# Float32r scores in one pass of 32 rows, and exponentials over three PSUM banks

## The chip, the cores and the metric

The kernel runs on one core of a Trainium2 chip. The metric is the device time of one execution in microseconds. Before the change it took 10,427.56 us (median of 3 runs, 10,423.74 to 10,437.85).

Names of engines in the profile: PE is TensorE (PEld its weight loads), ACT is ScalarE, DVE is VectorE, POOL is GpSimd, and SP is SyncE, which issues most of the DMAs here. PSUM has eight banks of 512 float32 columns on 128 partitions. PE writes its results there and the other engines fetch them.

## The reference

Four images of 64 x 64 pixels with 128 channels go through two layers, all in float32.

```python
# layer 0: gated convolutions and causal attention, one head of 4 (q, k) and 16 (v) dims
c1 = conv_same(elu(x), W1, b1)
a, b = split(conv_same(c1, W2, b2), 2)
c3 = a * sigmoid(b)
q, k, v = c3 @ Wq + bq, c3 @ Wk + bk, c3 @ Wv + bv
x = x + c3 + tile(causal_softmax(q @ k.T / 4) @ v, 8) @ W3 + b3
# layer 1: t holds 4096 tokens of 128 dims
y = layernorm(t); q, k, v = y @ wq, y @ wk, y @ wv      # 16 heads of 8 dims
h = y + (softmax(q @ k.T) @ v) @ wo                     # no mask: 4096 x 4096 scores a head
t = t + h + (silu(h @ w1) * (h @ w3)) @ w2
y = layernorm(t)                                        # 8 experts, the best two of each token
t = t + sum_of_top2(softmax(y @ router_w + router_b), y @ expert_w + expert_b)
```

Most of the arithmetic is in layer 1's attention: 4 images x 16 heads x 4096 x 4096 scores, one exponential for each, and their weighted sums.

## The kernel before

`fast_path` computes one image after the other. Exponentials are taken of the bare scores; at the end a verdict on the largest queries, keys and values says whether that was safe, and only if not does `general_path` compute everything again. Here it does not.

Per image the stages are `l0_convs` (L244 to L308), `l0_attention` (scores L402, exponentials L415 and L418, sums L381, `project` L358), the transposes of the normalised tokens, `l1_attention` (from L430), `l1_ffn` (L567) and `l1_experts` (L601).

**Layer 1's attention.** Its first part projects queries and keys for eight blocks of 512 tokens (L438, L439). To keep float32 accuracy with bf16 products, `three_terms` (L235 to L242) splits the result into three bf16 terms: an ACT cast, a DVE subtraction, a POOL cast and another DVE subtraction. The terms go to DRAM (`d_k`, `d_q`) and come back with each row in the right place: for each of four heads (NSLOT), 24 rows at partition 32j. The rows of keys are the 8 dims times 3 key terms. The rows of queries hold one dim three times, so that one matmul over 24 rows multiplies one query term with all three key terms. Three matmuls into the same PSUM columns (L546, i = 0, 1, 2) give all nine products.

The main loop walks 32 blocks: four groups g of four heads, and for each eight blocks c of 512 queries. In each block it takes 32 steps kt, one per 128 keys. A step has
- 12 bf16 score matmuls of 24 rows x 128 keys x 512 queries (three terms, four heads; the heads stand in different 32-row groups of the array), into two tiles of two PSUM banks each,
- two exponentials of 128 x 1024 (L556) on ACT,
- four float32 sums `acc += v1.T @ e` (L509; two matmul instructions each in the trace), one per head, in four 32-column groups of the array. Their 9 rows are a row of ones and 8 dims of v, so that the softmax's denominator comes along.

The sums lag LAG = 2 steps behind the scores. At a block's end DVE copies `acc` to SBUF (L524). Two steps later `by_token` transposes it on PE (L495) and normalises on DVE (L498, L500). Keys of the next group (`keys`, four DMAs) and queries of the next block (`queries`, four DMAs) are loaded one ahead into second buffers by SP.

**PSUM.** One bank holds `acc`, one is `m_tile` for small products and transposes, and six belong to the pool `ps_s`: three buffers of two banks. All stages take their tiles from it by `s_tile()`: convolutions, layer 0's scores and its projection, the FFN's two products (L583, L584), the experts' products (L666, which DVE adds up in L675).

**What orders the work.** A framework orders the instructions of each engine, and it puts a semaphore wait ahead of an instruction where a buffer that it reads or writes is still in use by another engine. Which buffer a tile gets is settled by its pool. Each engine works through its own list in order; a waiting instruction holds up those behind it.

Of the kernel before, what the change touches and what calls it, by code (L numbers as in the profile page):

```python
# [8 lines left out]

FP = mybir.dt.float32  # L10
BF = mybir.dt.bfloat16
AF = mybir.ActivationFunctionType
ALU = mybir.AluOpType
AX = mybir.AxisListType

P = 128
C = 128
IMG = 64
N = IMG * IMG
NT = N // P  # L20
QB = 512
NQ = N // QB
# [4 lines left out]
SLOT = 32  # L27
NSLOT = P // SLOT
# [5 lines left out]
HIDDEN = 344  # L34
FCH = [(0, 128), (128, 128), (256, 88)]
NE = 8

NTERM = 3  # L40
# [49 lines left out]
def fast_path(ctx: ExitStack, tc: tile.TileContext, a: dict, where: dict, out: bass.AP, verdict):  # L90
# [2 lines left out]
    x = a["x"]  # L93
    B = x.shape[0]
    LAG = 2

    const = ctx.enter_context(tc.tile_pool(name="f_const", bufs=1))
    big = ctx.enter_context(tc.tile_pool(name="f_big", bufs=1))
    ep = ctx.enter_context(tc.tile_pool(name="f_ep", bufs=8))
    wk = ctx.enter_context(tc.tile_pool(name="f_wk", bufs=2))  # L100
    sm = ctx.enter_context(tc.tile_pool(name="f_sm", bufs=2))
    dram = ctx.enter_context(tc.tile_pool(name="f_dram", bufs=2, space=bass.MemoryType.DRAM))
    ps_s = ctx.enter_context(tc.tile_pool(name="f_ps_s", bufs=3, space=bass.MemoryType.PSUM))
    ps_o = ctx.enter_context(tc.tile_pool(name="f_ps_o", bufs=1, space=bass.MemoryType.PSUM))
    ps_m = ctx.enter_context(tc.tile_pool(name="f_ps_m", bufs=1, space=bass.MemoryType.PSUM))

    def s_tile():
        return ps_s.tile([P, 1024], FP, tag="s", name="s")

    def m_tile():  # L110
        return ps_m.tile([P, QB], FP, tag="m", name="m")

    def e_tile():
        return ep.tile([P, 1024], FP, tag="e", name="e")


    n_fast = where["head_sum"][1]
# [116 lines left out]
    def three_terms(src):  # L234

        xs = wk.tile([P, NTERM, 1024], BF, tag="x", name="x")
        rest = e_tile()
        nc.scalar.copy(xs[:, 0, :], src)
        nc.vector.tensor_tensor(rest, src, xs[:, 0, :], ALU.subtract)
        nc.gpsimd.tensor_copy(xs[:, 1, :], rest)  # L240
        nc.vector.tensor_tensor(xs[:, 2, :], rest, xs[:, 1, :], ALU.subtract)
        return xs  # L242
# [186 lines left out]

    def l1_attention(b, yT, h):  # L430

        d_k = dram.tile([P, NTERM, N], BF, tag="k1", name="d_k1")
        d_q = dram.tile([NQ, P, NTERM, QB], BF, tag="q1", name="d_q1")
        top = sm.tile([P, 2, NQ], FP, tag="top", name="top")
        for c in range(NQ):
            cols = slice(c * QB, (c + 1) * QB)
            ps = s_tile()
            nc.tensor.matmul(ps[:, :QB], lhsT=wq1, rhs=yT[:, cols], start=True, stop=True)  # L438
            nc.tensor.matmul(ps[:, QB:], lhsT=wk1, rhs=yT[:, cols], start=True, stop=True)  # L439
            nc.vector.tensor_reduce(  # L440
                top[:, :, c], ps.rearrange("p (j n) -> p j n", j=2), AX.X, ALU.max, apply_absolute_value=True
            )
            terms = three_terms(ps)
            nc.sync.dma_start(out=d_k[:, :, cols], in_=terms[:, :, QB:])
            nc.sync.dma_start(out=d_q[c], in_=terms[:, :, :QB])

        tops = sm.tile([P, 2], FP, tag="tops", name="tops")
        nc.vector.tensor_reduce(tops, top, AX.X, ALU.max)
        nc.vector.tensor_tensor(seen[:, 2, b : b + 1], tops[:, 0:1], tops[:, 1:2], ALU.mult)
        nc.vector.tensor_scalar(seen[:, 2, b : b + 1], seen[:, 2, b : b + 1], 1e30, None, ALU.min)  # L450

        top_v = sm.tile([P, NT // 8], FP, tag="topv", name="topv")
        for s in range(NT // 8):
            ps = s_tile()
            for k in range(8):
                i = 8 * s + k
                nc.tensor.matmul(
                    ps[:, k * P : (k + 1) * P], lhsT=yT[:, i * P : (i + 1) * P], rhs=wv1, start=True, stop=True
                )
            nc.vector.tensor_copy(  # L460
                v1[:, 8 * s : 8 * s + 8, :, 1:], ps.rearrange("p (k h d) -> p k h d", h=NH1, d=HD1)
            )
            nc.vector.tensor_reduce(top_v[:, s : s + 1], ps, AX.X, ALU.max, apply_absolute_value=True)
        nc.vector.tensor_reduce(seen[:, 3, b : b + 1], top_v, AX.X, ALU.max)


        rows = HD1 * NTERM

        def keys(g):
            kx = big.tile([P, N], BF, tag="kx", bufs=2, name="kx")  # L470
            for j in range(NSLOT):
                head = NSLOT * g + j
                src = d_k[head * HD1 : (head + 1) * HD1].rearrange("d y n -> (d y) n")
                nc.sync.dma_start(out=kx[j * SLOT : j * SLOT + rows, :], in_=src)
            return kx

        def queries(g, c):

            qx = wk.tile([P, NTERM, QB], BF, tag="qx", name="qx")
            for j in range(NSLOT):  # L480
                head = NSLOT * g + j
                src = d_q[c][head * HD1 : (head + 1) * HD1].rearrange("d x n -> d (x n)")
                nc.sync.dma_start(
                    out=qx[j * SLOT : j * SLOT + rows].rearrange("p x n -> p (x n)"),
                    in_=src.unsqueeze(1).to_broadcast([HD1, NTERM, NTERM * QB]),
                )
            return qx

        nt = big.tile([P, NT, C], FP, tag="y", name="nt")

        def by_token(g, c, at):

            ps = m_tile()
            for k in range(4):
                nc.tensor.transpose(ps[:, k * P : (k + 1) * P], at[:, k * P : (k + 1) * P], ident)  # L495
            pj = ps.rearrange("p (k j s) -> p k j s", j=NSLOT, s=SLOT)
            rc = sm.tile([P, 4, NSLOT], FP, tag="rc", name="rc")
            nc.vector.reciprocal(rc, pj[:, :, :, 0])  # L498
            gc = slice(g * NSLOT * HD1, (g + 1) * NSLOT * HD1)
            nc.vector.tensor_tensor(  # L500
                nt[:, 4 * c : 4 * c + 4, gc].rearrange("p k (j d) -> p k j d", d=HD1),
                pj[:, :, :, 1 : 1 + HD1],
                rc.unsqueeze(3).to_broadcast([P, 4, NSLOT, HD1]),
                ALU.mult,
            )

        def add_up(g, c, kt, es):
            for j in range(NSLOT):
                nc.tensor.matmul(  # L509
                    acc[j * SLOT : j * SLOT + 1 + HD1, :],  # L510
                    lhsT=v1[:, kt, NSLOT * g + j, :],
                    rhs=es[j // 2][:, (j % 2) * QB : (j % 2 + 1) * QB],
                    start=kt == 0,
                    stop=kt == NT - 1,
                )

        order = [(g, c) for g in range(NG1) for c in range(NQ)]
        ready = []

        def finish(n, kt, es):  # L520
            add_up(*order[n], kt, es)
            if kt == NT - 1:
                at = wk.tile([P, QB], FP, tag="at", name="at1")
                nc.vector.tensor_copy(at, acc)  # L524
                ready.append(at)
            if kt == 1 and ready:
                by_token(*order[n - 1], ready.pop())

        kx, qx = keys(0), queries(0, 0)
        kx_next = qx_next = None  # L530
        late = []
        for n, (g, c) in enumerate(order):
            if n:
                qx = qx_next
                if c == 0:
                    kx = kx_next
            if n + 1 < len(order):
                qx_next = queries(*order[n + 1])
            if c == 0 and g + 1 < NG1:
                kx_next = keys(g + 1)  # L540
            for kt in range(NT):
                ss = [s_tile(), s_tile()]
                for i in range(NTERM):
                    for j in range(NSLOT):
                        r = slice(j * SLOT, j * SLOT + rows)
                        nc.tensor.matmul(  # L546
                            ss[j // 2][:, (j % 2) * QB : (j % 2 + 1) * QB],
                            lhsT=kx[r, kt * P : (kt + 1) * P],
                            rhs=qx[r, i, :],
                            start=i == 0,  # L550
                            stop=i == NTERM - 1,
                        )
                es = []
                for ps in ss:
                    e = e_tile()
                    nc.scalar.activation(e, ps, AF.Exp)  # L556
                    es.append(e)
                late.append((n, kt, es))
                if len(late) > LAG:
                    finish(*late.pop(0))  # L560
        for item in late:
            finish(*item)
        by_token(*order[-1], ready.pop())
        return nt

# [847 lines left out]
```

## Time and profile before

| | us |
|---|---|
| median of 3 runs | 10,427.56 |
| the profiled execution | 10,433.93 |
| its span | 10,432.1 |
| PE busy | 9,972.6 |
| ACT busy | 8,198.4 |
| DVE busy | 1,150.2 |
| the four attentions of layer 1, first to last exponential | 4 x 1,932 |

A stage is a stretch of the timeline. In the first image the convolutions take until about 245 us, layer 0's attention until 376, the projection until 418, layer 1's attention until 2,352, the FFN until 2,500 and the experts until 2,627; the next images repeat this every 2,600 us.

In a group of the profile, the text before the bar is line, engine, operation, result and operands, shapes and count; behind it are busy time in us and the mean ns of one; behind the second bar is the idle time of the engine just before these instructions, and what ended it. The durations of neighbouring instructions on PE and ACT overlap somewhat, so that the distance of two starts is shorter than one duration. PEclk or "granted clock" is the share of TensorE's full clock that the chip granted.

### The profile page before, as it was taken

The numbers are of one execution on the slowest core, as the hardware profiler recorded it, in microseconds if no ns is written. First come the engines' busy times: TensorE is split into PE (matmuls) and PEld (weight loads), VectorE is DVE, ScalarE is ACT, GpSimd is POOL, SyncE is SP. The second block draws the span as 40 slices with busy tenths as digits, with TensorE's granted clock in tenths as the row PEclk, the third lists the DMA queues.
The fourth block names the chain that finished last, engine by engine and source line by source line (L and its number), as shares of the span: only waits on it lengthen the run. The fifth ranks groups of instructions, "written<-read, shape, count | busy, mean of one in ns | idle before, by whom it ended". The sixth has DMA issues, their size and how long they took to land.

```text
span 10432.1 us, 204188 instructions
## 1 busy us (share of the span) xinstructions
PE 9972.6 (96%) x90561; PEld 3179.9 (30%) x90565; DVE 1150.2 (11%) x3539; ACT 8198.4 (79%) x8965; POOL 184.3 (2%) x177
## 2 busy tenths in 40 slices
PE   8899999997989999999798999999979899999997
PEld 4322222224432222222442222222244222222224
DVE  1200000004220000000412000000051200000005
ACT  1699999991169999999116999999911799999991
POOL 0000000000000000000000000000000000000000
PEclk9999999998999999999889999999988999999998
DMA  1100000000010000000001000000000100000000
GB/s 26 35 6 10 6 9 7 6 5 15 5 34 6 10 6 9 7 6 5 16 4 35 7 9 6 10 6 6 5 16 4 35 7 9 6 10 6 6 5 9
DMA packets 86914, 112.51 MB, mean 11 GB/s; under 512 B 8835, under 2 KB 71779, under 8 KB 84195
## 3 DMA queue, kind: packets, MB, share of 16 engines
q1 hardware_dynamic: 83267, 97.59, 3.2%
q8 instruction: 710, 11.63, 0.5%
q10 hardware_dynamic: 2752, 1.77, 0.1%
q14 instruction: 185, 1.52, 0.0%
HBM read 64.99 MB, written 34.34 MB: 10 GB/s over the span
## 4 chain that ended last, share of the span: by engine, by line
PE 93%; DVE 4%; DMA 1%; ACT 1%; issue 0%; SPq 0%; POOL 0%; DVEq 0%; ACTq 0%; POOLq 0%
PE acc L509 38%; PE s L546 35%; PE s L291 5%; PE s L276 2%; PE s L666 2%; PE acc L381 2%; DVE t L675 2%; PE s L402 1%; PE s L583 1%; PE s L584 1%; PE m L495 1%; PE m L592 1%; PE m L231 1%; PE s L367 1%; PE m L574 0%
## 5 line engine op out<-in xcount | busy, mean ns | idle before, releaser
L556 ACT ACTIVATE e<-s 128x1024 f32<-128x1024 f32 x8192 | 7642.7, 1022 | 149.5 <-PE s L546 149.5
L509 PE MATMUL acc<-e,f_v 128*9 128x512 f32 x32768 | 4296.2, 595 | 4.5 <-ACT e L556 4.5
L546 PE MATMUL s<-qx,kx 24*128 24x512 bf16 x49152 | 3926.0, 377 | 29.5 <-DMA kx<-d_k 28.5
L546 PEld LDWEIGHTS <-kx 24*128 24x128 bf16 x49152 | 1548.0, 91 | 3823.5 <-issue 3467.2
L509 PEld LDWEIGHTS acc<-e,f_v 128*9 128x9 f32 x32768 | 486.7, 88 | 1753.4 <-issue 1687.1
L524 DVE COPY at<-acc 128x512 f32<-128x512 f32 x128 | 88.6, 692 | 7149.6 <-PE acc L509 7149.6
L291 PE MATMUL s<-c,f_w2c 128*128 128x512 f32 x1152 | 499.9, 592 | 0.0
L666 PE MATMUL s<-f_we,e 128*128 128x512 f32 x512 | 313.1, 763 | 58.2 <-DVE t L675 53.2
L299 ACT ACTIVATE e<-s,f_b 128x512 f32<-128x512 f32 x32 | 22.0, 687 | 422.8 <-PE s L291 422.7
L675 DVE SCALAR_TENSOR_TENSOR t<-s,gate,t 128x128 f32<-128x128 f32 x1024 | 305.9, 343 | 5.3 <-PE s L666 2.5
L291 PEld LDWEIGHTS s<-c,f_w2c 128*128 128x128 f32 x1152 | 215.5, 189 | 263.5 <-issue 263.5
L418 ACT ACTIVATE e<-s 128x1024 f32<-128x1024 f32 x224 | 217.6, 1021 | 91.1 <-PE s L402 90.4
L276 PE MATMUL s<-e,f_w1c 128*128 128x512 f32 x576 | 249.9, 596 | 3.1 <-DVE t L675 1.9
L402 PE MATMUL s<-qk 36*128 36x512 bf16 (+1 forms) x576 | 169.3, 388 | 76.0 <-DMA qk<-d_q 74.1
L655 ACT COPY g<-m 8x512 f32<-8x512 f32 x32 | 18.4, 575 | 230.4 <-PE m L653 230.4
L232 ACT COPY e<-m 128x512 f32<-128x512 f32 x64 | 37.5, 586 | 204.4 <-PE m L231 204.4
L381 PE MATMUL acc<-e,f_v 128*17 128x512 f32 (+3 forms) x1152 | 197.7, 600 | 0.0
L586 ACT ACTIVATE e<-s 128x512 f32<-128x512 f32 (+1 forms) x96 | 56.8, 596 | 165.6 <-PE s L584 165.5
L588 POOL TENSOR_TENSOR t<-t,h 128x512 f32<-128x512 f32 x32 | 40.5, 1266 | 8117.7 <-DVE h L577 8117.7
L666 PEld LDWEIGHTS s<-f_we,e 128*128 128x128 f32 x512 | 118.7, 247 | 202.9 <-issue 120.9
L283 ACT ACTIVATE c<-s,f_b 128x1024 f32<-128x1024 f32 x16 | 17.9, 1118 | 186.7 <-PE s L276 186.7
L276 PEld LDWEIGHTS s<-e,f_w1c 128*128 128x128 f32 x576 | 109.2, 190 | 141.7 <-issue 141.0
(146 smaller groups left out, 2962.0 us busy)
## 6 DMA issues: line engine op xcount, KB each, us to landing
qx<-d_q SPq DMA_DIRECT2D x512, 72.0 KB
d_k<-x SPq DMA_DIRECT2D x32, 384.0 KB
d_q<-x SPq DMA_DIRECT2D x32, 384.0 KB
kx<-d_k SPq DMA_DIRECT2D x64, 192.0 KB
t<-in_x_dram SPq DMA_DIRECT2D x16, 512.0 KB
out_dram<-t SPq DMA_DIRECT2D x32, 256.0 KB
f_w2c<-in_L_conv_W_dram ACTq DMA_DIRECT2D x1, 1152.0 KB
qk<-d_q SPq DMA_DIRECT2D x12, 96.0 KB
```

Of the source, the lines that this page charges most:

```text
L231: nc.tensor.transpose(ps[:, k * P : (k + 1) * P], src[:, k, :], ident)
L276: nc.tensor.matmul(rows(ps[:, h * QB : (h + 1) * QB]), lhsT=w1c[:, tap, :], rhs=e0[:, r0 : r0 + 8, kx : kx + IMG], start=(tap == 0), stop= ...
L291: nc.tensor.matmul(rows(ps[:, h * QB : (h + 1) * QB]), lhsT=w2c[:, tap, h * C : (h + 1) * C], rhs=c1[:, 8 * c + ky : 8 * c + ky + 8, kx : ...
L367: nc.tensor.matmul(ps[:, k * C : (k + 1) * C], lhsT=l_, rhs=w3f, start=True, stop=True)
L381: nc.tensor.matmul(acc[j * SLOT : j * SLOT + 1 + DV0, off:], lhsT=v0[:, kt, :], rhs=e[:, lo:hi], start=r == 0, stop=r == c,)
L402: nc.tensor.matmul(ps[:, lo:hi], lhsT=kx[:kr, kt * P : (kt + 1) * P], rhs=qx[:kr, c * QB + off : (c + 1) * QB], start=True, stop=r < c,)
L418: nc.scalar.activation(e, ps, AF.Exp)
L509: nc.tensor.matmul(acc[j * SLOT : j * SLOT + 1 + HD1, :], lhsT=v1[:, kt, NSLOT * g + j, :], rhs=es[j // 2][:, (j % 2) * QB : (j % 2 + 1) * ...
L546: nc.tensor.matmul(ss[j // 2][:, (j % 2) * QB : (j % 2 + 1) * QB], lhsT=kx[r, kt * P : (kt + 1) * P], rhs=qx[r, i, :], start=i == 0, stop= ...
L556: nc.scalar.activation(e, ps, AF.Exp)
L666: nc.tensor.matmul(px[:, h * QB : (h + 1) * QB], lhsT=yT[:, k * P : (k + 1) * P], rhs=we_f[:, h * QB : (h + 1) * QB], start=True, stop=True,)
L675: nc.vector.scalar_tensor_tensor(tk, px[:, n * C : (n + 1) * C], gate[:, k, n : n + 1], tk, ALU.mult, ALU.add)
```

## The change

- Queries and keys are split into two terms of the type float32r (`FR`; four bytes): an ACT copy that rounds, and a DVE subtraction. The POOL cast and one of the two DVE subtractions go. `d_k` and `d_q` hold four-byte values; `d_q` is written twice over.
- Rows: 8 dims x 2 key terms x 2 make 32 rows per head, which hold all four products of the terms. One matmul of 32 rows replaces the three of 24 rows. The four heads fill all 128 rows.
- Keys of a group come in four DMAs of a quarter of the tokens each, into one buffer `kx` instead of two. Queries of a block come in one DMA.
- Scores are numbered through over heads, steps and blocks, and taken three at a time (WIDE = 3): three scores into three neighbouring PSUM banks, one exponential of 128 x 1536. A triple can span two steps or two blocks. There are 5,464 exponentials instead of 8,192. A step's four sums are issued when the score of its last head is handed over. The buffers for exponentials are five of 1536 columns instead of eight of 1024.
- The six PSUM banks are one tile, `banks`, for the whole kernel. `s_tile(n)` gives the next n banks of it in turn. All stages use it.

```diff
-    ep = ctx.enter_context(tc.tile_pool(name="f_ep", bufs=8))
+    ep = ctx.enter_context(tc.tile_pool(name="f_ep", bufs=5))
...
-    ps_s = ctx.enter_context(tc.tile_pool(name="f_ps_s", bufs=3, space=bass.MemoryType.PSUM))
+    ps_s = ctx.enter_context(tc.tile_pool(name="f_ps_s", bufs=1, space=bass.MemoryType.PSUM))
...
-    def s_tile():
-        return ps_s.tile([P, 1024], FP, tag="s", name="s")
+    banks = ps_s.tile([P, 6, QB], FP, tag="s", name="s")
+    turn = [0]
+    def s_tile(n=2):
+        at = turn[0] if turn[0] + n <= 6 else 0
+        turn[0] = at + n
+        return banks[:, at : at + n, :].rearrange("p b n -> p (b n)")
...
-            terms = three_terms(ps)
+            terms = wk.tile([P, 2, 1024], FP, tag="x", name="two")
+            nc.scalar.copy(terms[:, 0, :].bitcast(FR), ps)
+            nc.vector.tensor_tensor(terms[:, 1, :].bitcast(FR), ps, terms[:, 0, :], ALU.subtract)
             nc.sync.dma_start(out=d_k[:, :, cols], in_=terms[:, :, QB:])
-            nc.sync.dma_start(out=d_q[c], in_=terms[:, :, :QB])
+            for y in range(2):
+                nc.sync.dma_start(out=d_q[c][:, y], in_=terms[:, :, :QB])
...
+        kx = big.tile([P, N], FP, tag="kx", bufs=1, name="kx")
         def keys(g):
-            kx = big.tile([P, N], BF, tag="kx", bufs=2, name="kx")
-            for j in range(NSLOT):
...
+            src = d_k[g * SLOT : (g + 1) * SLOT].rearrange("d y n -> (d y) n")
+            for s in range(4):
+                cols = slice(s * N // 4, (s + 1) * N // 4)
+                nc.sync.dma_start(
+                    out=kx[:, cols], in_=src[:, cols].unsqueeze(1).to_broadcast([2 * SLOT, 2, N // 4])
+                )
...
+        work = [(n, kt, j) for n in range(len(order)) for kt in range(NT) for j in range(NSLOT)]
...
+        for first in range(0, len(work), WIDE):
+            now = work[first : first + WIDE]
+            ps = s_tile(WIDE)
+            for i, (n, kt, j) in enumerate(now):
...
+                r = slice(j * SLOT, (j + 1) * SLOT)
+                nc.tensor.matmul(
+                    ps[:, i * QB : (i + 1) * QB],
+                    lhsT=kx[r, kt * P : (kt + 1) * P].bitcast(FR),
+                    rhs=qx[r, :].bitcast(FR),
+                    start=True,
+                    stop=True,
+                )
...
+            e = ep.tile([P, WIDE * QB], FP, tag="e", name="e")
+            nc.scalar.activation(e[:, : len(now) * QB], ps[:, : len(now) * QB], AF.Exp)
+            late.append([(w, e[:, i * QB : (i + 1) * QB]) for i, w in enumerate(now)])
+            if len(late) > LAG:
+                late_now = late.pop(0)
...
+            for (n, kt, j), part in late_now:
+                have[j] = part
+                if j == NSLOT - 1:
+                    add_up(n, kt, have)
```

More of the change, by code (lines that the diff above doesn't have):

```diff
@@ L11 @@
 BF = mybir.dt.bfloat16
+FR = mybir.dt.float32r
 AF = mybir.ActivationFunctionType
@@ L95, in fast_path @@
     LAG = 2
+    WIDE = 3
     const = ctx.enter_context(tc.tile_pool(name="f_const", bufs=1))
     big = ctx.enter_context(tc.tile_pool(name="f_big", bufs=1))
-    ep = ctx.enter_context(tc.tile_pool(name="f_ep", bufs=8))
+    ep = ctx.enter_context(tc.tile_pool(name="f_ep", bufs=5))
     wk = ctx.enter_context(tc.tile_pool(name="f_wk", bufs=2))
@@ L113, in e_tile @@
     def e_tile():
-        return ep.tile([P, 1024], FP, tag="e", name="e")
+        return ep.tile([P, WIDE * QB], FP, tag="e", name="e")[:, :1024]
     n_fast = where["head_sum"][1]
@@ L430, in l1_attention @@
     def l1_attention(b, yT, h):
-        d_k = dram.tile([P, NTERM, N], BF, tag="k1", name="d_k1")
-        d_q = dram.tile([NQ, P, NTERM, QB], BF, tag="q1", name="d_q1")
+        d_k = dram.tile([P, 2, N], FP, tag="k1", name="d_k1")
+        d_q = dram.tile([NQ, P, 2, 2, QB], FP, tag="q1", name="d_q1")
         top = sm.tile([P, 2, NQ], FP, tag="top", name="top")
@@ L464, in l1_attention @@
         nc.vector.tensor_reduce(seen[:, 3, b : b + 1], top_v, AX.X, ALU.max)
-        rows = HD1 * NTERM
+        kx = big.tile([P, N], FP, tag="kx", bufs=1, name="kx")
         def keys(g):
-            kx = big.tile([P, N], BF, tag="kx", bufs=2, name="kx")
-            for j in range(NSLOT):
[L472 to L475, printed above, removed]
-        def queries(g, c):
[L479 to L486, printed above, removed]
+            src = d_k[g * SLOT : (g + 1) * SLOT].rearrange("d y n -> (d y) n")
[4 more added lines that the diff above has]
+                )
+        def queries(g, c):
+            qx = wk.tile([P, QB], FP, tag="qx", name="qx")
+            nc.sync.dma_start(out=qx, in_=d_q[c][g * SLOT : (g + 1) * SLOT].rearrange("d y x n -> (d y x) n"))
             return qx
@@ L505, in by_token, with add_up @@
             )
-        def add_up(g, c, kt, es):
+        order = [(g, c) for g in range(NG1) for c in range(NQ)]
+        ready = []
+        def add_up(n, kt, es):
+            g, c = order[n]
             for j in range(NSLOT):
@@ L511, in add_up @@
                     lhsT=v1[:, kt, NSLOT * g + j, :],
-                    rhs=es[j // 2][:, (j % 2) * QB : (j % 2 + 1) * QB],
+                    rhs=es[j],
                     start=kt == 0,
@@ L515, in add_up @@
                 )
[L517 to L521, printed above, removed]
             if kt == NT - 1:
@@ L527, in finish @@
                 by_token(*order[n - 1], ready.pop())
[L529 to L560, printed above, removed]
@@ L561, in l1_attention @@
-        for item in late:
-            finish(*item)
+        work = [(n, kt, j) for n in range(len(order)) for kt in range(NT) for j in range(NSLOT)]
+        late, qx, qx_next = [], None, queries(0, 0)
+        have = {}
+        keys(0)
+        for first in range(0, len(work), WIDE):
+            now = work[first : first + WIDE]
+            ps = s_tile(WIDE)
+            for i, (n, kt, j) in enumerate(now):
+                if kt == 0 and j == 0:
+                    qx = qx_next
+                    if n + 1 < len(order):
+                        qx_next = queries(*order[n + 1])
+                r = slice(j * SLOT, (j + 1) * SLOT)
[6 more added lines that the diff above has]
+                )
+                g, c = order[n]
+                if c == NQ - 1 and kt == NT - 1 and j == NSLOT - 1 and g + 1 < NG1:
+                    keys(g + 1)
+            e = ep.tile([P, WIDE * QB], FP, tag="e", name="e")
[3 more added lines that the diff above has]
+                late_now = late.pop(0)
+            else:
+                late_now = []
+            if first + WIDE >= len(work):
+                late_now += [w for ws in late for w in ws]
+            for (n, kt, j), part in late_now:
+                have[j] = part
+                if j == NSLOT - 1:
+                    add_up(n, kt, have)
```

## The prediction

> **What bounds the kernel now.** I read the page first: busy time and the chain that ended last.
>
> ```profile
> PE 9972.6 (96%) x90561; PEld 3179.9 (30%) x90565; DVE 1150.2 (11%) x3539; ACT 8198.4 (79%) x8965; POOL 184.3 (2%) x177
> ...
> PE acc L509 38%; PE s L546 35%; PE s L291 5%; PE s L276 2%; PE s L666 2%; PE acc L381 2%; DVE t L675 2%; PE s L402 1%; PE s L583 1%; PE s L584 1%; PE m L495 1%; PE m L592 1%; PE m L231 1%; PE s L367 1%; PE m L574 0%
> ```
>
> Layer 1's attention (scores L546, sums L509) is 73% of the chain. Next, its stage alone, cut from the middle of the first image (us, busy time and count of each engine, granted clock, DMA share, GB/s):
>
> ```profile
> 480.00:1000.00 520.00, 520.00 (x5562) 140.83 (x5564) 11.17 (x27) 515.36 (x554) 0.00 (x0) 1.00 0.03 8
> ```
>
> PE is busy all the time and ACT 99% of it, both at once: 554 exponentials in 520 us make 1.877 us per step of two. They can run side by side because scores go to one pair of PSUM banks while ACT reads another. The prices, from the groups by line and shape:
>
> ```profile
> L556 ACT ACTIVATE e<-s 128x1024 f32<-128x1024 f32 x8192 | 7642.7, 1022 | 149.5 <-PE s L546 149.5
> L509 PE MATMUL acc<-e,f_v 128*9 128x512 f32 x32768 | 4296.2, 595 | 4.5 <-ACT e L556 4.5
> L546 PE MATMUL s<-qx,kx 24*128 24x512 bf16 x49152 | 3926.0, 377 | 29.5 <-DMA kx<-d_k 28.5 <-ACT e L556 1.0
> L675 DVE SCALAR_TENSOR_TENSOR t<-s,gate,t 128x128 f32<-128x128 f32 x1024 | 305.9, 343 | 5.3 <-PE s L666 2.5
> L524 DVE COPY at<-acc 128x512 f32<-128x512 f32 x128 | 88.6, 692 | 7149.6 <-PE acc L509 7149.6
> L495 PE MATMUL m<-f_consts,at 128*128 128x128 f32 x512 | 83.9, 286 | 3.2 <-DVE at L524 3.2
> L586 ACT ACTIVATE e<-s 128x512 f32<-128x512 f32 x64 | 37.8, 597 | 130.2 <-PE s L584 130.2
> ```
>
> The last view is the timeline where engines wait for one another outside attention (start, us, engine):
>
> ```profile
> 2356.32 0.59 ACT L232 COPY an<-m 128x512 f32<-128x512 f32 x1 [3.97 <-PE m L231]
> 2356.95 1.45 PEld L574 LDWEIGHTS m<-f_wo,an 128*128 128x128 f32 x8 [0.91 <-ACT an L232]
> ...
> 2359.48 1.12 PE L231 MATMUL m<-f_consts,h 128*128 128x128 f32 x4 [0.78 <-DVE h L577]
> ...
> 2360.69 0.59 ACT L232 COPY e<-m 128x512 f32<-128x512 f32 x1 [3.79 <-PE m L231]
> ```
>
> From ACT's end to PE's start is about 50 ns (51 in the unrounded records), from PE's end to ACT's start about 90 (92 to 102, where a semaphore instruction stands first). These two prices are nowhere on the path of attention today.
>
> **The edit that decides: one PSUM tile.** The change makes three 2-bank tiles into one tile of six banks, `banks`, and hands out slices. In the changed kernel as built, the instruction list of PE runs through attention like this:
>
> ```
> 622 L546 Matmult s_85<-qx_1568,kx_1566 128x512 [waits Activation_49]
> 623 L546 Matmult s_85<-qx_1568,kx_1566 128x512 x2
> 624 L519 Matmult acc_163<-e_1584,f_v1_161 9x512 x3
> ```
>
> Every score names the same buffer. I looked up the semaphore values: in 5,460 of 5,464 triples the first score waits for the value that the exponential just before it sets, although it writes the other three banks. So scores of triple n+1 wait for exponential n, and exponential n+1 waits for those scores: ACT no longer runs beside the scores. Behind the waiting score on PE stand the sums of the same triple; they run beside the next exponential. Per triple:
>
> - Exponential of 1536 columns: 1022 ns for 1024, 597 for 512 (L586), so 0.830 per column and 1,447.
> - ACT's end to PE's start: 51.
> - The scores: three 32-row groups side by side, as the four 24-row groups are now. A bf16 score took 374 (median). The list shows no separate weight load before these, so the load comes after the wait too: the first of four transposes (L495) took 328 against 273 for those behind it, 55 to 56 more. 374 + 56 + 10 for the offset of the third group = 440. Float32r is nowhere in the trace. Its bounds: 374 with nothing added, and an fp32 instruction of the same size with its load not hidden, 668. I take 440, since these are single instructions as the bf16 ones are, where each fp32 sum is two.
> - PE's end to ACT's start, with two waits on the exponential: 97 (54 if only the shortest 37 and the 17 of a semaphore instruction count).
>
> 1,447 + 51 + 440 + 97 = 2,035 ns; bounds 1,926 and 2,263. PE's own work (440, and 975 for a phase of sums) fits with 0.62 us to spare. A step of four scores thus takes 2.71 us instead of 1.86.
>
> 5,464 triples x 2.034 = 11,114 us. Before, the four attentions took 7,728 from first to last exponential (1,932 each). **+3,386.** Fewer exponentials (5,464 for 8,192) and 12 score passes become four; neither is worth anything on this chain beyond what the sum has.
>
> **Block ends.** 128 times the first sum of a block waits for the copy of acc (last sum's start + 639, copy 692, + 53 = 1.38 us) and the scores queued behind it wait as well; four transposes (0.29 each, partly beside) come later. The 0.62 us of room per triple takes much of it. Bounds 20 and 100 us in all; I take +60, near the middle.
>
> **Other stages.** Their tiles are slices of the same buffer, so each PE fill now waits for the evacuation before it. Per image:
> - Convs: four evacuations by ACT (1,118 + 150) and eight by ACT and DVE (687 + 690 + 150 or so) that were hidden: +17, with the first transposes +20.
> - Layer 0's attention: 56 half steps of 1,017 + 51 + 10 + 216 + 374 + 97 = 1.77 us against about 0.95; part of the stage was bound by PE already, so +35 to +110; I take +75.
> - Projection: the scores' terms lose a POOL cast (1.04) and a DVE subtract (1.22) per block of 512 tokens, but write 1.5 MB instead of 0.75 (DMA was 55% busy there), and the tiles wait: +5 to +23; +14.
> - FFN: 24 tiles with ACT 0.6 + 0.1 and DVE 0.69 + 0.05 no longer beside PE: 35; bounds 25 and 40; +33.
> - Experts: 32 tiles, PE's 4 x 0.435 = 1.74 us no longer beside DVE's 8 x 0.343 = 2.75: 61 with handovers, 110 at half clock; +70.
>
> Sum 212 per image (145 to 303), **+850** in all (580 to 1,210).
>
> **At nothing:** the key loads, though there is one buffer now: each of the four chunk loads waits for its own last readers alone, and the next group reads it some 40 us or more later. The one query load per block has 60 us or more. SP, which issues both, has nothing else in attention.
>
> **Sum.** 10,433.9 (the profiled execution; span 10,432.1, 6 us above the median 10,427.6 of the runs, so 0.06%) + 3,386 + 60 + 850 = **14,730 us**, +41%.
>
> **The clock.** Attention had 1.00 before. It was lower where PE idled often: in the FFN,
>
> ```profile
> 2370.00:2380.00 10.00, 6.96 (x37) 5.32 (x37) 2.86 (x11) 1.17 (x2) 2.29 (x2) 0.72 0.01 2
> ...
> 2390.00:2400.00 10.00, 6.96 (x35) 4.33 (x34) 3.55 (x12) 1.77 (x3) 2.28 (x2) 1.00 0.00 0
> ```
>
> the same 70% busy went with 0.72 and with 1.00. Afterwards attention's PE would be (430 + 975) / 2,034 = 69% busy. Finer: in stretches of 3.4 us, counting only streaming (215 ns a bf16 pass, 435 an fp32 one), all 71 falls to half came where PE streamed 0.41 or less; the new loop streams (215 + 870) / 2,034 = 0.53. I take full clock, with little room.
>
> The Trainium skill, "TensorE: Matmul & The Clock Gate", section "HAM oscillation — how this bites in real kernels", says that the clock falls for idle gaps above some 3.4 us; by it nothing would fall, but in the FFN gaps of 0.7 to 0.9 us went with it. Its section "A second HAM failure mode: psum-queue depth-cycling" speaks against this change: waiting through PSUM banks, with short idle times at each, made the clock swing; by that rule the clock rival below would be the forecast.
>
> The skill's "PSUM — Partial Sum Buffer", section "Terms", has engines collide only on the same bank and quadrant; by it the scores could run beside the exponential as they do now, and the sum would be that of the first rival. The wait is in the program, and I go by that.
>
> **Rivals.**
> 1. *Faster: the wait does not bind*, because it is met by an earlier exponential than I read. Then ACT's pitch decides: exponentials follow each other 108 ns before the last one's end now, so 1.34 us, unless PE's 1.38 (scores 0.40, sums 0.975) binds: 5,464 x 1.38 = 7,540, less 7,728 = -188; by 1.34, -406. 10,030 to 10,250. Below 7,728 / 5,464 = 1.414 us a triple the change gains. Against: the semaphore values. 3%.
> 2. *Float32r streams like fp32* (435 instead of 215): 2,034 + 220 = 2.254, x 5,464 = +1,202: 15,930. For: operands of four bytes. 10%.
> 3. *The clock halves*: at half clock (the first microseconds of attention had it) sums took 1.82 and a wave of scores 0.56, so PE's loop is 2.46 us and binds: +2,328, 17,060. But then PE is always busy, which brings the clock back; half the time gives 15,890. 10%.
> 4. *The three row groups run one after another*: +430, 17,080. Now four do run side by side. 4%.
> 5. My sum: 73%.
>
> **Numbers.** The likeliest is 14,730; its own range goes from 13,830 (all low bounds) to 15,300 (a load of weights and other stages at their high bounds). 8 in 10 needs rival 2 with other stages high (15,930 + 360) and the swinging clock: 13,850 to 16,300; left out are rival 1, rival 4, half of rival 3 and some tail, 18% together. A measurement can tell 0.2% from nothing. Slower 0.96 (all but rival 1), faster 0.03, same 0.01.
>
> **What would show it.** A group of 1536-wide exponentials, x5464, of 1,447 each, ACT 71% busy in attention and idle 0.59 us before each, put down to PE's scores; PE's scores idle, put down to ACT; first to last exponential 2,790 us per image. Exponentials back to back would show me wrong; scores of 590 ns rival 2; a granted clock under 1.00 there rival 3.

## The result, and the profile after

The changed kernel takes 15,670 us (median of four runs, 15,649 to 15,707) against 10,426: 1.503 times as long (95% interval 1.500 to 1.506). The forecast was 14,730 in a range of 13,850 to 16,300. Its profiled execution took 15,671.6 us, with a span of 15,669.8.

The page of the changed kernel, busy time, the clock that was granted in 40 slices, and the chain that ended last:

```profile
PE 11299.0 (72%) x57793; PEld 2912.9 (19%) x57797; DVE 1181.6 (8%) x3507; ACT 8495.8 (54%) x6237; POOL 150.0 (1%) x145
...
PEclk8899999997889999999788999999978899999997
...
ACT 50%; PE 39%; DVE 5%; issue 4%; another core or an unknown queue 1%; ACTq 1%; DMA 0%; SPq 0%; POOL 0%; DVEq 0%; POOLq 0%
ACT e L557 48%; PE s L546 19%; PE acc L519 4%; PE s L301 3%; PE s L672 3%; PE acc L391 2%; DVE t L681 2%; PE s L286 2%; PE s L412 1%; PE s L589 1%; ACT e L428 1%; PE m L241 1%; PE s L590 1%; DVE at L528 1%
```

Before, PE alone carried 93% of the chain. Now exponentials (L557) and scores (L546) share it, and the sums (L509 before, L519 now, 38% of the chain then) have nearly gone from it. They run beside an exponential; no score does so any more. The costliest groups say which waits there are (after the second bar, idle time in us and its cause):

```profile
L557 ACT ACTIVATE e<-s 128x1536 f32<-128x1536 f32 x5464 | 7919.6, 1449 | 3929.2 <-PE s L546 3929.2
L519 PE MATMUL acc<-e,f_v 128*9 128x512 f32 x32768 | 6009.0, 618 | 66.3 <-DVE at L528 66.3
L546 PE MATMUL s<-qx,kx 32*128 32x512 f32 x16384 | 2810.9, 506 | 3174.5 <-ACT e L557 3153.4
```

ACT waits 3,929 us for scores and PE's scores wait 3,153 us for ACT: two engines that wait for each other in turn. Before, the same two groups had 149.5 and 1.0. The timeline of the changed kernel shows one round (start, us, engine, instruction):

```profile
1498.79 1.45 ACT L557 ACTIVATE e<-s 128x1536 f32<-128x1536 f32 x1 [0.66 <-PE s L546]
1500.29 0.19 PEld L546 LDWEIGHTS s<-qx,kx 32*128 32x128 f32 x3 [1.56 <-ACT e L557]
1500.29 0.50 PE L546 MATMUL s<-qx,kx 32*128 32x512 f32 x3 [0.64 <-ACT e L557]
1500.72 0.11 PEld L519 LDWEIGHTS acc<-e,f_v 128*9 128x9 f32 x6 [0.25 <-issue]
1500.72 1.04 PE L519 MATMUL acc<-e,f_v 128*9 128x512 f32 x6
1500.90 1.45 ACT L557 ACTIVATE e<-s 128x1536 f32<-128x1536 f32 x1 [0.66 <-PE s L546]
```

The exponential ends at 1500.24, the next scores start at 1500.29 and end at 1500.79, the next exponential starts at 1500.90. A round is 2.11 us. The sums (1500.72 to 1501.76) hide in it and PE is idle 0.64 us.

Where the time came from, by stage, the four images added up. A stage ends where the next one's first matmul (or first exponential, or last one's end) is, and an image starts with its first transposes (L261 before, L271 now):

| stage | before | after | change | predicted |
|---|---|---|---|---|
| convolutions | 807 | 935 | +128 | +80 |
| layer 0's attention | 595 | 1,009 | +414 | +300 |
| projection | 214 | 330 | +116 | +56 |
| layer 1's attention | 7,732 | 11,748 | +4,016 | +3,446 |
| FFN | 553 | 634 | +81 | +132 |
| experts | 526 | 1,009 | +483 | +280 |

### The profile page after: what moved, and what is told of

It reads as the page before. It is cut to its first block, busy times and chain, and to the rows that moved or that the text cites. A ratio compares the mean times of both kernels' runs of the same rounds, so it can differ in the third digit from the quotient of the medians.

```text
span 15669.8 us, 132721 instructions
## 1 busy us (share of the span) xinstructions
PE 11299.0 (72%) x57793; PEld 2912.9 (19%) x57797; DVE 1181.6 (8%) x3507; ACT 8495.8 (54%) x6237; POOL 150.0 (1%) x145
## 4 chain that ended last, share of the span: by engine, by line
ACT 50%; PE 39%; DVE 5%; issue 4%; another core or an unknown queue 1%; ACTq 1%; DMA 0%; SPq 0%; POOL 0%; DVEq 0%; POOLq 0%
ACT e L557 48%; PE s L546 19%; PE acc L519 4%; PE s L301 3%; PE s L672 3%; PE acc L391 2%; DVE t L681 2%; PE s L286 2%; PE s L412 1%; PE s L589 1%; ACT e L428 1%; PE m L241 1%; PE s L590 1%; DVE at L528 1%
## 5 line engine op out<-in xcount | busy, mean ns | idle before, releaser
L557 ACT ACTIVATE e<-s 128x1536 f32<-128x1536 f32 x5464 | 7919.6, 1449 | 3929.2 <-PE s L546 3929.2
L519 PE MATMUL acc<-e,f_v 128*9 128x512 f32 x32768 | 6009.0, 618 | 66.3 <-DVE at L528 66.3
L546 PE MATMUL s<-qx,kx 32*128 32x512 f32 x16384 | 2810.9, 506 | 3174.5 <-ACT e L557 3153.4
L546 PEld LDWEIGHTS s<-qx,kx 32*128 32x128 f32 x16384 | 1047.6, 185 | 8362.4 <-ACT e L557 8269.3
L519 PEld LDWEIGHTS acc<-e,f_v 128*9 128x9 f32 x32768 | 624.7, 89 | 1528.5 <-issue 1378.4
L672 PE MATMUL s<-f_we,e 128*128 128x512 f32 x512 | 469.2, 1071 | 298.3 <-DVE t L681 298.3
L391 PE MATMUL acc<-e,f_v 128*17 128x512 f32 (+3 forms) x1152 | 444.5, 765 | 0.0
L428 ACT ACTIVATE e<-s 128x1024 f32<-128x1024 f32 x224 | 229.2, 1023 | 352.5 <-PE s L412 293.6
L412 PE MATMUL s<-qk 36*128 36x512 bf16 (+1 forms) x576 | 224.1, 459 | 183.5 <-DMA qk<-d_q 99.2
L589 PE MATMUL s<-e,f_fw 128*128 128x512 f32 (+1 forms) x192 | 120.6, 713 | 110.4 <-DVE gT L593 87.0
```

The source lines that it names most:

```text
L391: nc.tensor.matmul(acc[j * SLOT : j * SLOT + 1 + DV0, off:], lhsT=v0[:, kt, :], rhs=e[:, lo:hi], start=r == 0, stop=r == c,)
L412: nc.tensor.matmul(ps[:, lo:hi], lhsT=kx[:kr, kt * P : (kt + 1) * P], rhs=qx[:kr, c * QB + off : (c + 1) * QB], start=True, stop=r < c,)
L519: nc.tensor.matmul(acc[j * SLOT : j * SLOT + 1 + HD1, :], lhsT=v1[:, kt, NSLOT * g + j, :], rhs=es[j], start=kt == 0, stop=kt == NT - 1,)
L546: nc.tensor.matmul(ps[:, i * QB : (i + 1) * QB], lhsT=kx[r, kt * P : (kt + 1) * P].bitcast(FR), rhs=qx[r, :].bitcast(FR), start=True, stop ...
L557: nc.scalar.activation(e[:, : len(now) * QB], ps[:, : len(now) * QB], AF.Exp)
L589: nc.tensor.matmul(ps[:size, :QB], lhsT=fw1[:, lo : lo + size], rhs=hT, start=True, stop=True)
```

## The experiments

The prediction's theory was that one PSUM tile for all six banks makes every score wait for the exponential just before it, although other banks are written. Rivals were the float32r matmul, the clock, and the new order of the work.

### Two tiles of three banks

```diff
-    banks = ps_s.tile([P, 6, QB], FP, tag="s", name="s")
+    halves = [ps_s.tile([P, 3 * QB], FP, tag=f"s{i}", name=f"s{i}") for i in range(2)]
     turn = [0]
     def s_tile(n=2):
-        at = turn[0] if turn[0] + n <= 6 else 0
-        turn[0] = at + n
-        return banks[:, at : at + n, :].rearrange("p b n -> p (b n)")
+        turn[0] = 1 - turn[0]
+        return halves[turn[0]][:, : n * QB]
```

> The changed kernel with its six banks as two tiles of three banks, handed out in turn, instead of one tile of six. All else stays: float32r, one pass of 32 rows, exponentials of 1536. Theory (the single tile makes scores wait for the exponential just before): that wait is gone; ACT's exponentials follow each other every 1.34 us, or PE binds with 0.435 for the scores' phase, 0.87 to 0.975 for the sums and up to 0.1 for weight loads, 1.31 to 1.48. I take 1.40: 5464 x 1.40 = 7650 in the four attentions instead of 11,745, and the other stages go back to 2,690 and a little more, as they have two buffers instead of three: 10,250 to 10,700, around 10,400. Rival (the float32r matmul with its 181 ns weight load, or the clock, is what costs): the exponentials stay above 1.6 us apart and the time above 11,500.

It took 10,594 us, 1.0147 times before (1.0121 to 1.0173). 5,076 of the 5,244 us that the change had cost were gone, with float32r, triples, loads and order of the program untouched. Of the other stages, which came to 3,916 us after the change, 2,852 were left. Layer 1's attention went from 11,748 to 7,710. But that is no better than the 7,732 before: exponentials stand 1.41 us apart (mean) where 1.33 is the least that was seen. The timeline of this kernel shows what binds; below it is a stretch of its attention (us, busy time and count of PE, PEld, DVE, ACT and POOL, granted clock, DMA share, GB/s):

```profile
1508.95 0.51 PE L544 MATMUL s<-qx,kx 32*128 32x512 f32 x3
1509.39 0.12 PEld L517 LDWEIGHTS acc<-e,f_v 128*9 128x9 f32 x8 [0.25 <-issue]
1509.39 1.04 PE L517 MATMUL acc<-e,f_v 128*9 128x512 f32 x8
1510.37 0.19 PEld L544 LDWEIGHTS s<-qx,kx 32*128 32x128 f32 x3 [0.86 <-ACT e L555]
1510.37 0.50 PE L544 MATMUL s<-qx,kx 32*128 32x512 f32 x3
1510.80 0.10 PEld L517 LDWEIGHTS acc<-e,f_v 128*9 128x9 f32 x2 [0.24 <-issue]
1510.80 1.03 PE L517 MATMUL acc<-e,f_v 128*9 128x512 f32 x2
1511.76 0.19 PEld L544 LDWEIGHTS s<-qx,kx 32*128 32x128 f32 x3 [0.86 <-ACT e L555]
```

```profile
1000.00:1500.00 500.00, 494.58 (x3228) 108.89 (x3229) 10.68 (x26) 491.97 (x355) 0.00 (x0) 1.00 0.03 10
```

PE was busy for 494.6 of the 500 us; its scores and sums follow one another. A phase of all four heads' sums (x8, two instructions each) lasts from 1509.39 to the next scores at 1510.37, 0.98 us. A phase of one sum (x2) lasts from 1510.80 to 1511.76, 0.96 us. The scheduler had placed one sum of a step in one triple and three in the next.

### The kernel before with one tile

```diff
-    ps_s = ctx.enter_context(tc.tile_pool(name="f_ps_s", bufs=3, space=bass.MemoryType.PSUM))
+    ps_s = ctx.enter_context(tc.tile_pool(name="f_ps_s", bufs=1, space=bass.MemoryType.PSUM))
+    banks = ps_s.tile([P, 6, QB], FP, tag="s", name="s")
+    turn = [0]
     def s_tile():
-        return ps_s.tile([P, 1024], FP, tag="s", name="s")
+        at = turn[0] % 6
+        turn[0] += 2
+        return banks[:, at : at + 2, :].rearrange("p b n -> p (b n)")
```

> The kernel before with nothing changed but its PSUM: one tile of six banks, handed out in slices of two. Scores in bf16, 12 passes a step, exponentials of 1024. Theory (single tile): the first score of a step waits for both exponentials of the step before; a step is 1022 + 920 for two exponentials, 51, a scores' phase of 850 and 97, about 2.95 us instead of 1.88: +4,400 in attention; other stages as in the changed kernel, +1,220: about 16,000. Rival (float32r, the triples or the order of the work cost the time): within 3% of before, 10,400 to 10,750.

16,287 us, 1.559 times before (1.554 to 1.563). Not a single matmul or exponential differs from the kernel before, and the loss is larger than that of the whole change. Its timeline:

```profile
1499.85 1.94 ACT L561 ACTIVATE e<-s 128x1024 f32<-128x1024 f32 x2 [1.04 <-PE s L551]
...
1501.90 0.83 PE L551 MATMUL s<-qx,kx 24*128 24x512 bf16 x12
...
1502.83 1.94 ACT L561 ACTIVATE e<-s 128x1024 f32<-128x1024 f32 x2 [1.04 <-PE s L551]
```

ACT is idle 1.04 us before each pair; a step is 2.98 us (2.95 expected). The other stages came to 3,945 us, as the 3,916 of the changed kernel (2,695 before). So their share of the loss is the tile too.

### Float32r scores alone

In the kernel before, the two terms, the 32 rows, the loads and one matmul a score were put in; three tiles of two banks and pairs of 1024-wide exponentials stayed.

> The kernel before with the float32r scores alone: two terms, 32 rows, one matmul a score, one key buffer, one query load a block; three tiles of two banks and exponentials of 1024 as before. Theory: PE has 0.435 + 0.975 and perhaps 0.1 for loads in a step, 1.5 us at most, and ACT binds with two exponentials at 0.905 to 0.92: 1.81 to 1.84 a step instead of 1.888: -200 to -310, so 10,120 to 10,230. Rival (float32r scores cost more on PE than the 12 bf16 passes): above 10,430.

10,250.5 us beside 10,448.7 for before: 0.981 (0.979 to 0.984), -198 us. The expected gain of 200 to 310 was missed by 2 us. The time is 20 us above the expected range; before was itself 21 us slower in these runs than in those of the prediction. Attention took 7,539 us instead of 7,732 and ACT was busy all the time there: the distance of exponentials is 905 ns by the median, where a quarter of them had stood at 972 to 976 before.

```profile
500.00:1000.00 500.00, 500.00 (x3304) 134.83 (x3306) 9.93 (x24) 500.00 (x547) 0.00 (x0) 1.00 0.03 9
```

So the first half of the change is a gain, cut short by ACT: an exponential starts 0.59 us (median) after its scores have ended. But PE has no room either, against the expectation of 1.5 us a step at most. Its four scores go in two pairs of 0.43 us, one after the other, and with 0.98 for the sums that is 1.84 us a step, where two exponentials take 1.83.

### bf16 in place of float32r

The changed kernel, one tile, with `d_k`, `d_q`, `kx`, `qx` and the two terms in bf16.

> The changed kernel with the two terms rounded to bf16 instead of float32r, in the same 32 rows, one matmul a score (it leaves out the bits of the product below two bf16 terms). The PSUM tile stays one. In the changed kernel a score takes 504 ns from the end of the wait to the end of the matmul, of which its weight load shows 181. If the 4-byte weight load is what made it longer than the 440 that I had summed: load 91, matmul 385: a triple 2.00 us instead of 2.11, -600 us: about 15,070. If it is the matmul itself or the wait, no change beyond 100 us: 15,570 to 15,770.

14,991 us, 679 less (15,070 was expected). A round is 1.998 us instead of 2.111, as expected. The timeline shows the difference:

```profile
1500.66 0.09 PEld L546 LDWEIGHTS <-kx 32*128 32x128 bf16 x1 [0.86 <-issue]
1501.37 0.39 PE L546 MATMUL s<-qx,kx 32*128 32x512 bf16 x3 [0.64 <-ACT e L557]
```

The bf16 weight load is an instruction of its own without the wait, and ran 0.7 us ahead; the wait holds only the matmul, which takes 0.39 us. The float32r weight load carries the wait itself (its idle time above ends with ACT's exponential), takes 181 ns instead of 91, and the scores end 0.50 us after the wait. Attention took 711 us less, of which 5,464 x 0.113 = 617 are the rounds. Its clock stayed at full speed here, unlike in the changed kernel, and the other 94 us have the size of that (below).

### PE kept busy in the experts

```diff
+            with tc.issue_after(last.ins):
+                for _ in range(2):
+                    nc.tensor.matmul(acc, lhsT=yT[:, k * P : (k + 1) * P], rhs=we_f[:, :QB], start=True, stop=True)
             tk = t[:, 4 * c + k, :]
```

> The changed kernel with two more float32 matmuls of 128 x 512 behind the two of each expert tile, into the bank of acc, which nothing uses there; their results are thrown away. They add 2 x 0.87 = 1.74 us of PE work per tile, meant to run beside DVE's eight additions of 2.75 us, while PE would wait. In the changed kernel the experts take 252 us an image at a granted clock of 0.62 to 0.67, before 138 at 0.81. Theory (part of the experts' loss is the clock, which falls as PE idles): the clock there goes back to 0.9 or more, a tile's own matmuls take 1.74 us again instead of up to 3.5, and the experts take 195 to 215 us an image in spite of the added work: -150 to -230 in all, 15,440 to 15,520. Rival (the loss is the wait alone): 252 us or more, 15,670 or more.

15,449 us, 221 less, with more work. The experts took 811 us in all instead of 1,009. The experts' stretch of the first image, of the changed kernel and then of this one; the third line is that of the kernel before, with 7 us of the next image's transposes at its end (us; PE, PEld, DVE, ACT, POOL busy; granted clock, DMA share, GB/s):

```profile
3662.00:3914.00 252.00, 152.06 (x321) 66.49 (x320) 121.65 (x486) 12.39 (x25) 5.03 (x5) 0.66 0.03 8
```

```profile
3669.00:3871.00 202.00, 158.56 (x449) 73.94 (x450) 123.29 (x488) 12.40 (x25) 5.03 (x5) 0.92 0.03 10
```

```profile
2494.00:2632.00 138.00, 109.77 (x352) 57.79 (x352) 107.23 (x491) 17.44 (x31) 5.79 (x6) 0.81 0.05 14
```

Between the first two: 128 more PE instructions, 50 us less, and the clock at 0.92 instead of 0.66. An expert matmul took 704 ns instead of 1,071. So of the 483 us that the experts lost, some 200 go with the clock, which fell when PE began to wait.

### Two halves, and the sums kept together

```diff
+        def in_order(mm):
+            if before_it[0] is not None:
+                tc.add_manual_dep(mm.ins, before_it[0].ins.name, ...)
+            before_it[0] = mm
...
-                nc.tensor.matmul(
+                in_order(nc.tensor.matmul(
                     acc[j * SLOT : j * SLOT + 1 + HD1, :],
...
-                nc.tensor.matmul(
+                in_order(nc.tensor.matmul(
                     ps[:, i * QB : (i + 1) * QB],
```

> The kernel with two tiles of three banks, and attention's matmuls on PE held in the order of the program. Without that a step's four sums were split over two triples (1 and 3, 2 and 2, or 4), so that each of four triples had a phase of sums of 0.97 us, as long for one sum as for four, and PE had 0.44 + 0.97 = 1.41 us a triple. Theory (this split is why the halves did not gain): the four sums of a step stay together in three of four triples, PE has (4 x 0.44 + 3 x 0.97) / 4 = 1.17 us a triple, and ACT binds at the 1.33 that was its shortest distance: 5464 x 1.335 and the seams, 7,330 to 7,400 in attention instead of 7,707, so 10,220 to 10,290. Rival (two buffers are too few whatever the order): no change, 10,540 to 10,620.

10,231 us beside 10,428: 0.981 (0.977 to 0.984). Attention took 7,395 us, in the expected 7,330 to 7,400, and exponentials stand 1.330 us apart by the median. The timeline now has every fourth triple without sums, and PE waits for ACT there:

```profile
1509.15 0.50 PE L556 MATMUL s<-qx,kx 32*128 32x512 f32 x3
1510.36 0.19 PEld L556 LDWEIGHTS s<-qx,kx 32*128 32x128 f32 x3 [1.02 <-ACT e L567]
1510.36 0.51 PE L556 MATMUL s<-qx,kx 32*128 32x512 f32 x3 [0.71 <-ACT e L567]
1510.80 0.12 PEld L529 LDWEIGHTS acc<-e,f_v 128*9 128x9 f32 x8 [0.25 <-issue]
1510.80 1.05 PE L529 MATMUL acc<-e,f_v 128*9 128x512 f32 x8
```

### The banks shared out by stage

The order of the run before is kept (its lines are left out here).

```diff
+    def share(n):
+        stage.close()
+        ps_s[0] = stage.enter_context(tc.tile_pool(name=f"f_ps_s{n}", bufs=6 // n, space=bass.MemoryType.PSUM))
     def s_tile(n=2):
+        return ps_s[0].tile([P, n * QB], FP, tag="s", name="s")
...
+        share(WIDE)
         work = [(n, kt, j) for n in range(len(order)) for kt in range(NT) for j in range(NSLOT)]
...
         nt = l1_attention(b, yT, h)
+        share(2)
```

> The same with the six banks shared out anew for each stage: two tiles of three banks while layer 1's attention runs its main loop, three tiles of two banks, as in the kernel before, in all other stages. Theory: the other stages lose the wait of a missing third buffer, 2,853 back to about 2,700 us, unless the hand-over between the two layouts costs some us twice an image: 10,050 to 10,130. Rival (the hand-over drains the engines, or overlap between stages is lost): 10,200 or more.

10,065 us beside 10,428: 0.963 (0.961 to 0.966). This beats both kernels. The other stages came to 2,688 us (2,840 with two halves, 2,695 before), attention to 7,389. The hand-over costs nothing that shows. The stretch of attention that bounded the kernel before reads here:

```profile
480.00:1000.00 520.00, 460.20 (x3503) 110.08 (x3500) 11.17 (x27) 518.27 (x386) 0.00 (x0) 1.00 0.03 10
```

ACT is busy 99.7% of it and PE 88%: the bound has moved from PE and ACT together to ACT alone.

## Why the prediction was right, and where its sizes were off

**The number.** 15,670 is 940 above the forecast, and above the range of its own sum too, which ended at 15,300. It lies in the stated range through the room left for rival 2 and the swinging clock. Rival 2 did not come true and the clock only in small, so that much is luck; the excess comes from the sizes below.

**The edit that decides: one PSUM tile.** Right. Taking the single tile out of the changed kernel, and putting it into the kernel before, moved the time by 5,076 and by 5,838 us; nothing else that was tried moved it by more than 700. The Trainium skill, "PSUM — Partial Sum Buffer", section "Terms", has two engines collide when they are on the same bank and quadrant at once. The two-halves kernel agrees: scores ran there beside an exponential of other banks of the same partitions, with ACT busy 492.0 and PE 494.6 of 500 us. The wait in the changed kernel comes from how the program names its buffer, not from the banks.

**The round.** 2,111 ns measured, 2,035 summed. Term by term: exponential 1,450 (1,447), ACT's end to PE's start 53 (51), PE's end to ACT's start 105 (97), the scores 504 (440). The mis-sized term is the scores: I took a bf16 score of 374 and 56 for a weight load that comes after the wait, from the transposes' row. The bf16 run shows what the float32r score, with its load after the wait, costs more: 113 ns, twice what I took for the load. The load's own row is 181 ns against 91. With the two small terms that is 5,464 x 0.077 = 421 us of the 940 that were missing. It lay inside the bounds that I had given (1,926 to 2,263).

**Block ends, at +60, and the clock, at nothing.** Together they came to some 210 us. At a block's end the distance of two exponentials was 3.2, 3.2 and 2.87 us in turn, 0.98 more than a round on average, so 125 us for 128 block ends: the scores behind the sum that waits for the copy of acc come late by more than PE's idle time could take. The timeline of one:

```profile
1490.13 0.69 DVE L528 COPY at<-acc 128x512 f32<-128x512 f32 x1 [89.97 <-PE acc L519]
1490.87 0.10 PEld L519 LDWEIGHTS acc<-e,f_v 128*9 128x9 f32 x2 [1.72 <-DVE at L528]
1490.88 1.03 PE L519 MATMUL acc<-e,f_v 128*9 128x512 f32 x2 [0.79 <-DVE at L528]
1491.83 0.19 PEld L546 LDWEIGHTS s<-qx,kx 32*128 32x128 f32 x3 [0.86 <-issue]
...
1492.44 1.45 ACT L557 ACTIVATE e<-s 128x1536 f32<-128x1536 f32 x1 [1.76 <-PE s L546]
```

My bound of 100 us counted on that room. Here again a single sum (x2) holds PE for 0.95 us. Most of the remaining 85 us are the clock: rival 3 came true in small. Behind the stretch at its start, the attention of the four images had 34, 50, 45 and 50 stretches at half clock, nearly all of 3.4 us (642 us in all); the round in such a stretch took 2.45 to 2.55 us (the prediction had 2.46, though its two terms, 1.82 and 0.56, add up to 2.38). One such stretch and the next, and the scores and sums in the first:

```profile
1662.90:1666.30 3.40, 3.40 (x18) 0.52 (x15) 0.00 (x0) 2.13 (x2) 0.00 (x0) 0.51 0.00 0
1666.30:1669.70 3.40, 2.54 (x21) 0.52 (x18) 0.00 (x0) 2.21 (x2) 0.00 (x0) 0.99 0.00 0
```

```profile
1664.71 0.29 PEld L546 LDWEIGHTS s<-qx,kx 32*128 32x128 f32 x3 [1.70 <-ACT e L557]
1664.71 0.80 PE L546 MATMUL s<-qx,kx 32*128 32x512 f32 x3
1665.44 0.12 PEld L519 LDWEIGHTS acc<-e,f_v 128*9 128x9 f32 x6 [0.44 <-issue]
```

As I had argued, the half clock keeps PE busy all the time (3.40 of 3.40), and the full clock is back in the next stretch. I had full clock "with little room" and should have charged for the little.

**Other stages, at +850.** 1,221, just above the upper bound of 1,210. Layer 0's attention took 414 (300; bounds 140 and 440), the experts 483 (280; above their bound of 440), the convolutions 128 (80), the projection 116 (56; above its bound of 92), the FFN 81 (132; below its bound of 100). The term that was sized worst is the experts': I took 70 us an image, between 61 at full clock and 110 at half clock, and it was 121, more than either. With the wait the granted clock fell there from about 0.81 to between 0.62 and 0.67, and the run with added matmuls shows that about 200 of the 483 us go with it. In layer 0 it fell from 0.83 to between 0.68 and 0.76; how much of layer 0's and the projection's loss is the clock was not tried. In the FFN, where the forecast was too high, the clock went the other way, from 0.82 to 0.89 before to 0.86 to 0.98 now. So the wait does not lower the clock in every stage.

**The rivals.** Rival 1 (the wait does not bind) is out: PE's scores waited 3,153 us for it. Rival 2 (float32r at fp32's rate) is out: the sums follow 0.43 us after the start of the scores (1500.29 to 1500.72), in the bf16 run 0.32 us after (1501.37 to 1501.69), and the rival had 0.22 for this difference of 0.11. The stretches at half clock tell streaming and load apart. There the 0.43 became 0.73 (1664.71 to 1665.44), 0.29 more by the median, of which the weight load took 0.10 (181 to 283 ns); bf16's 0.32 became 0.54, 0.21 more. Four heads' float32 sums, two instructions each, went from 0.98 to 1.83 us in the run with the sums kept together, 0.42 more an instruction. So a float32r score streams like one of bf16. Rival 4 is out by the same numbers: three scores one after another would need three passes. The price of rival 1, 10,030 to 10,250, is where the repaired kernels came out (10,231 and 10,065), but only once the sums were kept together as well; with the wait alone taken away it was 10,594.

**At nothing:** the loads hid, as claimed: no wait for `kx` or `qx` is among the changed kernel's larger ones.

## What to carry to other kernels

A buffer is as fine as its dependency tracking: slices of one large PSUM tile that are meant to take turns can serialise the engines that they were to keep apart, so read which instruction each wait points to, and give each turn a tile of its own. When a change puts two engines in series, ask what the new waits do to the clock as well, stage by stage: here it fell in most of the stages that share the buffer and rose in one. And where small matmuls share the array side by side, one of them can cost as much time as the whole group, so keep a group together.

## What the runs showed of the hardware

- A float32r score of 32 x 128 x 512 streams like a bf16 one, but its weight load takes 181 ns against bf16's 91 and stands behind the wait of the matmul. Three side by side hold PE for 0.43 us, three of bf16, whose load ran ahead, for 0.32.
- One float32 sum into one column group holds PE for 0.96 us, four into four groups for 0.98.
- An exponential over three banks takes 1,450 ns alone, and one follows another every 1,330 ns.
- The clock fell to half in attention where PE was idle 0.64 us in every 2.11. The Trainium skill, "TensorE: Matmul & The Clock Gate", section "HAM oscillation — how this bites in real kernels", wants an idle gap above some 3.4 us for that; PE's longest in attention, behind its first 20 us, was 0.81 us. Its section "A second HAM failure mode: psum-queue depth-cycling" describes what was seen, an oscillation from short idle times between groups that wait for PSUM; here it cost about 85 us of 11,748, an estimate from the remainder above.
- Why the changed kernel's attention fell and that of the bf16 run did not, at the same idle time, fits a worst case rather than a mean. A stretch of 3.4 us holds one round and a piece of the next, and at worst this piece holds all the time in which nothing streams. With 215 + 870 = 1,085 ns of streaming a round, the least in 3.4 us is 0.40 of the time at 2.11 us a round and 0.46 at 2.00. In the trace of before, all falls had come at 0.41 or less. I had compared that limit with the mean over whole rounds, 0.53. The traces of the changed kernel and of the bf16 run bear the worst case out. The clock's changes lie on a grid of 3.41 us. By an estimate from the matmul rows (213 ns a score, 427 a float32 instruction, put 0.2 us ahead of the row's end), the changed kernel's attention streamed 0.382 to 0.389 of the time in the 178 stretches of this grid that stood just before a fall, and 0.395 to 0.767 in the other 3,052 at full clock; the bf16 run's streamed 0.44 at the least in 3,209. Put 0.06 us ahead of the end, the two ranges overlap by 0.03. No run of its own varied this share, and it is checked for attention alone.
